# The last sample's chain cut in halves over VectorE and ScalarE, with its logits made twice

## The chip, the core and the metric

The kernel runs on one core of one Trainium2 chip. The metric is the device time of one execution in microseconds (us), lower is better. TensorE (PE in the profile) multiplies matrices and turns tiles around, and writes to PSUM; VectorE (DVE) and ScalarE (ACT) read PSUM and write to SBUF; GpSimd (POOL) works on SBUF only; SyncE (SP) issues nearly all DMAs. Each engine works through its own instructions in order, and the engines wait for each other through semaphores.

## What is computed

The reference is a network of two layers on 16 samples of 128 channels by 32 x 32 places (1024 tokens of 128 channels), all in float32:

```
x = x + linear_attention(ln_c(x));   t = tokens(x);  t = t + spectral_filter(ln_t(t))      # layer 0
x = x + conv_block(ln_c(x));         t = tokens(x);  t = t + routed_experts(ln_t(t))       # layer 1

conv_block(u):  relu(bn(conv3x3(relu(bn(conv3x3(u))))) + u)
routed_experts(t):                     # t: 16 x 1024 x 128, 64 experts, K = 8
  probs  = softmax(t @ gate_w.T + gate_b, over the 1024 tokens)
  topv, topi = the 8 largest of each expert's 1024 probabilities
  pooled = sum over those 8 tokens of topv * token              # 16 x 64 x 128
  out    = gelu(pooled @ weight1 + bias1) @ weight2 + bias2     # one expert, one pair of matrices
  result[topi] += topv * out
```

Only layer 1 matters here, and of it the last of the 16 samples: from its second convolution to the moment when its pooled tokens are there, without which no expert can start.

## The kernel before, in words

Layer 0 fills the first half of the time. Layer 1 has three stages.

**Samples.** Every sample b runs through some seventy named steps, from `even` (the inverse transform of layer 0's filter) to `channels_copy`; every second sample (odd b) also runs the routing of its pair (b-1, b): `logits`, `largest`, `exp`, `replace`, `gates`, `turn`, `turn_copy`, `pool`, `pool_copy`, `pooled`, `pooled_copy`. The steps are methods of the class `Routed`. A table gives each step an engine, a cost, a due time and what it waits for; `planned` makes one list of all steps of all samples out of it. The loop under `manual_schedule` calls the methods in that list's order, and on each engine the instructions stand as they were called. With its list the planner works on two or three samples at once: while sample b is in its second convolution, sample b-1 is in its routing.

**The steps of the last sample (b = 15) that matter**, with the lines of the profile:

- `sums2` (L1218, L1219), `mids2` (L1226), `rows2` (L1232): VectorE gathers the second convolution (PE, L1013) into `yo`.
- `resid` (L1272) and `last` (L1278): VectorE adds the residual, applies relu, and adds the sample's own `x` (the tile `xp`); 1024 elements each.
- `tokens2` (PE, L152): eight transposes turn `x` into tokens, into a PSUM tile `big`. `stats2` (DVE, L135): four `bn_stats`, for the mean and the variance of each token.
- `copy2` (ACT, L1291): copies the tokens into the SBUF tile `tt`. `variance2` (POOL, L1294), `root2` (ACT, L121 and L122) and `scales2` (DVE, L127 to L129 and L1090) make a scale and a shift for each token; `norm2` (ACT, L144, eight instructions) applies them to `tt` in place.
- `channels` (PE, L172) turns the normalised tokens back; `channels_copy` (ACT, L1312) copies them into `tk`.
- `logits` (PE, L1320): four matmuls, for two halves of 512 tokens and for both samples of the pair, into one `big` tile `pl` (experts of sample 14 on partitions 0 to 63, of sample 15 on 64 to 127).
- `largest` (DVE, L1328 to L1331): the eight largest logits of each row, and the shift for the exponential. `replace` (DVE, L1341): marks those eight in a copy `lr`. `exp` (ACT, L1335): exponential of `pl` into `eg`, with its sum. `gates` (DVE, L1344 and L1347): keeps the exponential where `lr` is marked; a reciprocal of the sum.
- `turn` (PE, L152), `turn_copy` (ACT, L1360): gates with tokens on partitions, in `gtt`. `pool` (PE, L1367): 16 matmuls of gates by tokens. `pool_copy` (DVE, L1374), `pooled` (PE, L1380), `pooled_copy` (DVE, L1384).

Two things run beside these steps. `keep` issues matmuls on the identity whose result nobody reads (`wm`, L165), so many behind a step as the dictionary `idle` says. And a PSUM tile is tracked as a whole: where two engines touch one `big` tile (two banks of PSUM), the later in program order waits for the earlier, also if both only read.

**Experts.** 16 groups of four experts: `hidden` (PE, L1555 for the bias and L1564; gelu on ACT, L1570), `turn` (PE, L1578; DVE, L1580), `output` (PE, L1589; DVE, L1594), `collect` (PE, L1600; DVE, L1601). The weights of a group are two halves of 1 MB; there are 32 halves, in a ring of 14 places. A half is loaded when the group before it in its place has been used (`load_half`). Ahead of the first group ScalarE makes `ob` (L1610, eight instructions: the second bias times each pair's `rs`) in the place of `lr`, and loads the table for gelu.

**Outputs.** Two matmuls by sample half spread the experts' results over the tokens (L1649), VectorE, or ScalarE and GpSimd, add them to `x` (L1656, L1657, L1659), and a DMA of 512 KB by sample writes them out (L1660). The gates of earlier pairs and ten of the samples come back from memory for this (`gt`, L1492; `xb`, L965). The loads of gates are issued behind `logits`, and wait for the places `tk` (free after `logits`) and `tt` (free after `pool`).

Of the kernel before, what the change touches and what calls it, by code (L numbers as in the profile page):

```python
# [8 lines left out]
F32 = mybir.dt.float32  # L9
AF = mybir.ActivationFunctionType  # L10
ALU = mybir.AluOpType
# [3 lines left out]
P = 128  # L15
B, C, H, W = 16, 128, 32, 32
N = H * W
# [52 lines left out]
def metaformer_kernel(ctx: ExitStack, tc: tile.TileContext, io: dict, out: bass.AP):  # L70
# [70 lines left out]
    def normalize(dst, src, r, nm, lo=0, hi=NT):  # L141

        for j in range(lo, hi):
            nc.scalar.activation(  # L144
                dst[:, j, :], src[:, j, :], AF.Identity,
                bias=nm[:, j : j + 1], scale=r[:, j : j + 1],
            )
# [29 lines left out]
    with ExitStack() as l0:  # L177
# [43 lines left out]
        with ExitStack() as a0:  # L221
# [121 lines left out]
            def big():  # L343
                return ps.tile([P, N], F32, name="big", tag="big", bufs=3)
# [6 lines left out]
            def small(shape, name):  # L351
                return work.tile(shape, F32, name=name, tag=name, bufs=5)
# [3 lines left out]
            class Attention:  # L356


                def __init__(self, b):
                    self.b = b  # L360
                    self.sts = small([P, 4, NT], "sts")
                    self.sts2 = small([P, 4, NT], "sts2")
                    self.ga = small([P, 4], "ga")
                    self.qs = small([P, 3], "qs")
                    self.ks = small([P, 2, NT * HEADS], "ks")

                def tokens(self):
                    if self.b + 2 < B:
                        load(self.b + 2)
                    self.x = xt[self.b]  # L370
                    self.pt = big().rearrange("p (j c) -> p j c", c=C)
                    transpose_in(self.pt, self.x)
# [45 lines left out]
                def channels(self):  # L418
                    self.px = big()
                    transpose_out(self.px, self.tok)  # L420
# [145 lines left out]
                def norm2(self):  # L566
                    normalize(self.ub, self.ub, self.sts2[:, 0], self.sts2[:, 3])
# [367 lines left out]
    with ExitStack() as c1:  # L935
# [83 lines left out]
        def big():  # L1019
            return ps.tile([P, N], F32, name="big", tag="big", bufs=2)  # L1020

        idle = {(13, "turn"): 4, (13, "pooled"): 8, (15, "logits"): 11, (15, "turn"): 1}

        def tokens(t):
            return t.rearrange("p (j c) -> p j c", c=C)
# [69 lines left out]
        class Routed:  # L1095
# [57 lines left out]
            def copy(self):  # L1153
                self.tok = work.tile([P, NT, C], F32, name="tok", tag="tok", bufs=1)
                nc.scalar.copy(self.tok, self.pt)
# [120 lines left out]
            def last(self):  # L1276
                xv = self.x.rearrange("p (n o) -> p n o", o=4)
                nc.vector.scalar_tensor_tensor(  # L1278
                    xv, self.yo.rearrange("p o n -> p n o"), 0.0, xv, ALU.max, ALU.add
                )  # L1280
# [5 lines left out]
            def stats2(self):  # L1286
                self.stats()
# [99 lines left out]
                )  # L1387


        table = (  # L1390
            ("yin", "SP", 2.4, 10207.4, "", "y", ""),
            ("even", "POOL", 1.37, 11971.6, "yin", "z", ""),
# [97 lines left out]
        def load_gates(pr, tag, bufs):  # L1490
# [4 lines left out]
            table, buffers, B, 240.92, lambda b, name: b % 2 == 0 and name in pairs,  # L1495
            lambda b, name: 0.6 if name == "yin" and b else 0.0,
        )
        with tc.manual_schedule(engines=PINNED | {mybir.EngineType.SP}):
            for b in range(2):
                load(b)  # L1500
            for n in range(2):
                nc.sync.dma_start(cw[n], cwd[n])
            bs = w1[:, C, :].rearrange("(k r i) h -> r k i h", r=2, i=EG)
            for r in range(2):
                nc.sync.dma_start(b1[r * E // 2 : (r + 1) * E // 2, :], bs[r])
            for j in range(2):
                nc.sync.dma_start(b2[j * E : (j + 1) * E, :], w2[:, HID, :])
            samples = [None] * B
            keep(ps, "cv", 26)
            for b, name in order:  # L1510
                if name == "yin":
                    if b > 1:
                        load(b)
                    continue
                if samples[b] is None:
                    samples[b] = Routed(b)
                arg = args.get(name, (name,))
                getattr(samples[b], arg[0])(*(
                    getattr(samples[b], a) if a in ("va", "vb") else a for a in arg[1:]
                ))  # L1520
                if name == "tokens2":
                    if b // 2 in AWAY:
                        nc.sync.dma_start(xd[b], samples[b].x)
                    if b % 2 == 0 and b // 2 - 1 in AWAY:
                        load_half(b // 2 - 1 - AWAY[0])
                keep(ps, "cv", idle.get((b, name), 0))
                if b == B - 1 and name == "inverse":
                    for h in range(5, 9):
                        load_half(h)
                elif b == B - 1 and name == "convc":  # L1530
                    load_half(9)
                elif b == B - 1 and name == "last":
                    for h in range(10, len(RING)):
                        load_half(h)
                elif b == B - 1 and name == "logits":
                    for pr in range(2):
                        load_gates(pr, "tk", 2)
                    for pr in range(2, 4):
                        load_gates(pr, "tt", 4)
# [276 lines left out]
```

## Time and profile before

The median of four runs is 1234.5 us (1231.87, 1233.5, 1235.51, 1237.07). The profiled execution is the last of these.

| | |
|---|---|
| profiled execution's own time | 1237.07 us |
| its span in the profile | 1235.3 us |
| busy share of the span: PE, PE's weight loads, DVE, ACT, POOL | 94%, 77%, 75%, 59%, 49% |
| mean granted clock of TensorE | 0.986 |
| DMA moved, mean over the span | 142 GB/s |
| last `sums2` of sample 15 begins (DVE, L1218) | 1113.37 us |
| first gelu begins (ACT, L1570) | 1146.80 us |
| first output DMA issued (SP, L1660) | 1211.28 us |

Times are from the start of the span. A row of a timeline gives start and duration of a group of like instructions, and in brackets how long the engine had idled before it and what ended the idling. A row of a table by stretches gives, for each engine, the busy time and (x) the number of instructions, then the clock that TensorE was granted (1.00 is full speed), the share of the 16 DMA engines that was busy, and GB/s.

### The profile page before, as it was taken

To read this page: it belongs to the slowest core of one execution; us is meant where nothing else is said; L and a number is where in the kernel's file an instruction comes from. 1 tells how busy PE (TensorE), PEld (TensorE's weight loads), DVE (VectorE), ACT (ScalarE), POOL (GpSimd) and SP (SyncE) were. 2 spreads that over 40 slices of the span, in tenths; PEclk is the share of its full clock that TensorE was granted. 3 is DMA by queue.
4 is the path that set the end of the run, shared out by engine and by line. 5 is a ranking of instruction groups with operands and counts; after the bars stand their busy time and mean duration, and the time that the engine had idled before them with its cause. 6 is when DMAs were issued, how large, how long until landed. Compare 5 with 4: busy or idle time off the path is not lost.

```text
span 1235.3 us, 34369 instructions
## 1 busy us (share of the span) xinstructions
PE 1162.6 (94%) x14376; PEld 952.3 (77%) x14376; DVE 929.4 (75%) x1944; ACT 725.2 (59%) x1420; POOL 602.0 (49%) x800
## 2 busy tenths in 40 slices
PE   7889999999998999999997999999999999998996
PEld 4676767777777999999996888888888888885443
DVE  5888888887776677777764789898898989884335
ACT  4777777776655777777761346555556555644211
POOL 2436454654568788888882434343333334320003
PEclk9989999999999999999998999999999999999998
DMA  7014435253445244444448412233332331416998
GB/s 281 24 31 152 137 98 166 91 165 118 137 136 180 84 137 141 140 135 138 140 141 285 116 52 66 81 94 119 119 105 86 102 103 51 154 34 239 353 404 334
DMA packets 91243, 175.14 MB, mean 142 GB/s; under 512 B 5968, under 2 KB 42064, under 8 KB 90448
## 3 DMA queue, kind: packets, MB, share of 16 engines
q1 hardware_dynamic: 90448, 170.46, 41.5%
q0 software_dynamic: 640, 2.49, 0.6%
q8 instruction: 113, 1.85, 0.6%
q14 instruction: 42, 0.34, 0.1%
HBM read 110.28 MB, written 62.65 MB: 140 GB/s over the span
## 4 chain that ended last, share of the span: by engine, by line
PE 53%; DVE 22%; issue 11%; ACT 5%; DMA 5%; POOL 3%; SPq 0%; POOLq 0%; ACTq 0%; DVEq 0%
PE pcv L1013 10%; PE pg L817 9%; PE py L841 9%; PE big L639 6%; DVE bst L135 4%; PE big L172 3%; PE big L152 3%; PE big L571 3%; PE big L451 2%; PE big L534 2%; PE big L433 2%; DVE abss L1256 1%; DVE xp L1278 1%; DVE xp L1140 1%; ACT tt L144 1%
## 5 line engine op out<-in xcount | busy, mean ns | idle before, releaser
L1013 PE MATMUL pcv<-v,cw 128*128 128x256 f32 x1152 | 258.2, 380 | 1.6 <-POOL v L1203 1.6
L1013 PEld LDWEIGHTS pcv<-v,cw 128*128 128x128 f32 x1152 | 214.7, 190 | 34.7 <-issue 4.9
L828 DVE COPY g<-pg 128x512 f32<-128x512 f32 x196 | 127.8, 683 | 69.8 <-PE pg L817 69.8
L830 ACT COPY g<-pg 128x512 f32<-128x512 f32 x316 | 161.1, 605 | 28.3 <-PE pg L817 27.5
L817 PE MATMUL pg<-ph,mst 32*128 32x128 f32 x4096 | 139.1, 278 | 1.4 <-DVE x L646 0.9
L817 PEld LDWEIGHTS pg<-ph,mst 32*128 32x128 f32 x4096 | 126.3, 186 | 15.5 <-DVE g L828 8.7
L841 PE MATMUL py<-g,v 128*32 128x128 f32 x4096 | 126.1, 276 | 2.8 <-POOL v L809 1.8
L841 PEld LDWEIGHTS py<-g,v 128*32 128x32 f32 x4096 | 109.1, 111 | 10.8 <-POOL v L809 2.3
L144 ACT ACTIVATE tok<-tok,sts 128x128 f32<-128x128 f32 x256 | 101.9, 480 | 17.0 <-DVE sts L1090 13.6
L135 DVE BATCH_NORM_STATS2 bst<-big 128x6 f32<-128x256 f32 x256 | 91.2, 418 | 20.8 <-PE big L152 11.7
L808 POOL TENSOR_TENSOR v<-xc 128x256 f32<-128x256 f32 x128 | 97.1, 783 | 13.1 <-DMA xc<-vd 12.2
L639 PE MATMUL big<-u,mu 128*128 128x128 f32 (+4 forms) x384 | 86.0, 380 | 0.0
L1203 POOL TENSOR_TENSOR v<-abss 128x256 f32<-128x256 f32 x64 | 49.1, 786 | 68.1 <-DVE abss L1199 56.7
L287 POOL TENSOR_TENSOR xf<-ab 128x256 f32<-128x256 f32 x34 | 24.8, 728 | 113.5 <-DVE ab L254 113.4
L1222 POOL TENSOR_TENSOR yo<-abss 128x256 f32<-128x256 f32 x32 | 23.5, 736 | 108.6 <-DVE abss L1218 108.6
L639 PEld LDWEIGHTS big<-u,mu 128*128 128x128 f32 x384 | 56.7, 191 | 18.0 <-issue 15.4
L571 PE MATMUL big<-wf,ub 128*128 128x256 f32 x256 | 63.3, 391 | 0.2
L144 ACT ACTIVATE tt<-tt,sts 128x128 f32<-128x128 f32 x128 | 51.1, 481 | 14.5 <-DVE sts L1090 14.5
L809 POOL TENSOR_SCALAR v<-v 128x256 f32<-128x256 f32 x64 | 55.1, 861 | 5.6
L476 POOL TENSOR_TENSOR ke<-ke,ks 128x1024 f32<-128x1024 f32 x16 | 30.6, 1915 | 55.0 <-DVE qs L484 43.4
L915 ACT COPY yt<-py 128x512 f32<-128x512 f32 x60 | 35.2, 586 | 32.6 <-ACT g L830 16.3
L571 PEld LDWEIGHTS big<-wf,ub 128*128 128x128 f32 x256 | 46.9, 193 | 9.0 <-ACT xn L424 3.0
(256 smaller groups left out, 2489.3 us busy)
## 6 DMA issues: line engine op xcount, KB each, us to landing
we<-in_weight SPq DMA_DIRECT2D x32, 1024.0 KB, 9.3
xc<-vd SPq DMA_DIRECT2D x64, 256.0 KB, 3.2
yd<-ys SPq DMA_DIRECT2D x32, 512.0 KB, 3.8
vd<-xf SPq DMA_DIRECT2D x15, 1024.0 KB, 5.1
y<-yd SPq DMA_DIRECT2D x15, 896.0 KB, 6.8
x<-in_x SPq DMA_DIRECT2D x16, 512.0 KB, 5.1
mi<-in_M_phi SPq DMA_DIRECT2D x16, 512.0 KB, 4.7
xd<-x SPq DMA_DIRECT2D x16, 512.0 KB, 6.4
```

Source lines behind the costliest of these rows:

```text
L135: nc.vector.bn_stats(bst[:, j : j + 2, :].rearrange("p j s -> p (j s)"), src[:, j : j + 2, :].rearrange("p j c -> p c j"),)
L144: nc.scalar.activation(dst[:, j, :], src[:, j, :], AF.Identity, bias=nm[:, j : j + 1], scale=r[:, j : j + 1],)
L571: nc.tensor.matmul(dst, self.ub[:, q, :], wf[:, q, :], start=True, stop=True)
L639: nc.tensor.matmul(self.pa[:, a:hi], mu[:, NF - 1 - si, tap, :], self.u[:, a - tap : hi - tap], start=(tap == 0), stop=(tap == KU - 1),)
L808: nc.gpsimd.tensor_tensor(vv[:, x, 1:, bs], e, o, op)
L809: nc.gpsimd.tensor_scalar(v[:, :, 0, bs], v[:, :, 2, bs], -1.0, None, ALU.mult)
L817: nc.tensor.matmul(pg[r][:, i], mst[rs, 4 * q + i, :], ph[rs, c, :], start=True, stop=True,)
L828: nc.vector.tensor_copy(dst, src)
L830: nc.scalar.copy(dst, src)
L841: nc.tensor.matmul(py[rows, x, kl, :], v[:, (x * NM + m) * JL + jl, 1 - ri : 3 - ri, :] .rearrange("p k b -> p (k b)"), g[:, ((x * 2 + ri) ...
L1013: nc.tensor.matmul(pc[:, i], wt[:, dy, k, :], v[:, k, dy * WT : dy * WT + HT], start=(dy == 0), stop=(dy == 2),)
L1203: nc.gpsimd.tensor_tensor(v[:, k, WT : WT + HT], self.ab[:, 0], self.ab[:, 1], op)
```

## The change

The change touches the last sample only (and, of samples 13 and 14, the place of some steps in the list). A class `Final` takes the place of `Routed` for b = 15.

- `resid` and `last` become one step that works in two halves of 512 elements, with the transposes of each half behind it; the statistics of the first half are taken ahead of the second half's transposes.
- `copy2` is gone: the normalisation reads PSUM and writes `tt`, five of eight instructions on VectorE, three on ScalarE.
- `channels` goes into two small PSUM tiles of one bank each; VectorE copies one, ScalarE the other.
- `logits` are made twice, into two tiles. The maximum and the replacement read one, the exponential the other. The maximum is taken over two halves and then over the 16 results.
- The gates are made, turned and copied in halves; ScalarE copies the first half, VectorE the second. `gtt` takes the place of `tok` instead of `lr`.
- Ten steps are moved in the list: `exp` ahead of `replace`, `root2` ahead of where `copy2` stood; of sample 13, `pool_copy` and `pooled` behind `stats2` of sample 15 and `pooled_copy` behind its `scales2`; of sample 14, `scales2` and `norm2` behind `mids2` of sample 15, `channels` behind its `tokens2`, `channels_copy` behind its `root2`.
- `idle`: 2 instead of 8 unread matmuls behind `pooled` of sample 13, and 7 instead of 11 behind the last `logits`.

In the built program, the instructions and waits of all engines are the same up to the last `sums2`. Behind it, the transposes of the second half wait for the first half's two `bn_stats`; ScalarE's three normalisations wait for VectorE's fifth; the first `max` waits for all four matmuls of the first logits; four of the eight `ob` stand ahead of ScalarE's copy of the gates, and wait for the second half of `gates`; the transposes of the second half of the gates wait for that copy, VectorE's copy of them too.

```diff
@@ -1019,7 +1019,7 @@
         def big():
             return ps.tile([P, N], F32, name="big", tag="big", bufs=2)
 
-        idle = {(13, "turn"): 4, (13, "pooled"): 8, (15, "logits"): 11, (15, "turn"): 1}
+        idle = {(13, "turn"): 4, (13, "pooled"): 2, (15, "logits"): 7, (15, "turn"): 1}
 
         def tokens(t):
             return t.rearrange("p (j c) -> p j c", c=C)
@@ -1385,6 +1385,110 @@
                     pooled[:, :E, 2 * pr : 2 * pr + 2],
                     self.pp.rearrange("p (j e) -> p e j", j=2),
                 )
+
+
+        halves2 = (slice(0, HALF), slice(HALF, N))
+
+        class Final(Routed):
+
+
+            def __init__(self, b):
+                super().__init__(b)
+                self.bst = work.tile([P, NT, 3], F32, name="bst", tag="bst", bufs=5)
+
+            def nothing(self, *_):
+                pass
+
+            resid = tokens2 = copy2 = channels_copy = turn = turn_copy = nothing
+
+            def count(self, h):
+                for j in range(4 * h, 4 * h + 4, 2):
+                    nc.vector.bn_stats(
+                        self.bst[:, j : j + 2, :].rearrange("p j s -> p (j s)"),
+                        self.pt[:, j : j + 2, :].rearrange("p j c -> p c j"),
+                    )
+
+            def flip(self, dst, src, h):
+                for j in range(4):
+                    nc.tensor.transpose(dst[:, j, :], src[:, 4 * h + j], ident)
+
+            def last(self):
+                v = nc.vector
+                self.pt = tokens(big())
+                xj = self.x.rearrange("p (j c) -> p j c", c=P)
+                for h in range(2):
+                    ns = slice(h * HT // 2, (h + 1) * HT // 2)
+                    yo = self.yo[:, :, ns]
+                    v.scalar_tensor_tensor(
+                        yo, yo, bn[:, 1, 1:2], self.p1[:, :, ns], ALU.add, ALU.add
+                    )
+                    xv = self.x[:, halves2[h]].rearrange("p (n o) -> p n o", o=4)
+                    v.scalar_tensor_tensor(
+                        xv, yo.rearrange("p o n -> p n o"), 0.0, xv, ALU.max, ALU.add
+                    )
+                    if h:
+                        self.count(0)
+                    self.flip(self.pt[:, 4 * h : 4 * h + 4], xj, h)
+
+            def stats2(self):
+                self.count(1)
+                self.m, self.q = self.bst[:, :, 1], self.bst[:, :, 2]
+                self.sts = small([P, 4, NT], "sts")
+
+            def norm2(self, i):
+                if i:
+                    return
+                self.tt = toks[self.b] = work.tile([P, NT, C], F32, name="tt", tag="tt", bufs=4)
+                r, nm = self.sts[:, 0, :], self.sts[:, 3, :]
+                for j in range(5):
+                    nc.vector.tensor_scalar(
+                        self.tt[:, j], self.pt[:, j], r[:, j : j + 1], nm[:, j : j + 1],
+                        ALU.mult, ALU.add,
+                    )
+                normalize(self.tt, self.pt, r, nm, 5, NT)
+
+            def channels(self):
+                tks[self.b] = work.tile([P, N], F32, name="tk", tag="tk")
+                for h, copy in enumerate((nc.vector.tensor_copy, nc.scalar.copy)):
+                    pu = ps.tile([P, 4, P], F32, name="pu", tag="cv", bufs=3)
+                    self.flip(pu, self.tt, h)
+                    copy(tks[self.b][:, halves2[h]], pu.rearrange("p j c -> p (j c)"))
+
+            def logits(self):
+                super().logits()
+                one = self.pl
+                super().logits()
+                self.pl, self.pl2 = one, self.pl
+
+            def exp(self):
+                one, self.pl = self.pl, self.pl2
+                super().exp()
+                self.pl = one
+
+            def largest(self):
+                v = nc.vector
+                self.top = work.tile([P, TOPK], F32, name="top", tag="top")
+                two = work.tile([P, 2 * TOPK], F32, name="two", tag="two", bufs=1)
+                for h in range(2):
+                    v.max(two[:, h * TOPK : (h + 1) * TOPK], self.pl[:, halves2[h]])
+                v.max(self.top, two)
+                self.ss = work.tile([P, 3], F32, name="sm", tag="sm")
+                v.tensor_tensor(self.ss[:, 0:1], self.top[:, 0:1], gb, ALU.add)
+                v.tensor_tensor(self.ss[:, 1:2], gb, self.ss[:, 0:1], ALU.subtract)
+
+            def gates(self):
+                self.pg = tokens(big())
+                self.gtt = work.tile([P, NT, P], F32, name="gtt", tag="tok", bufs=1)
+                gj = self.gt.rearrange("p (j c) -> p j c", c=P)
+                for h, copy in enumerate((nc.scalar.copy, nc.vector.tensor_copy)):
+                    cs, js = halves2[h], slice(4 * h, 4 * h + 4)
+                    nc.vector.scalar_tensor_tensor(
+                        self.gt[:, cs], self.lr[:, cs], LOW, self.gt[:, cs], ALU.is_le, ALU.mult
+                    )
+                    self.flip(self.pg[:, js], gj, h)
+                    copy(self.gtt[:, js], self.pg[:, js])
+                nc.vector.reciprocal(rs[:, self.pr : self.pr + 1], self.ss[:, 2:3])
+                gates[self.pr] = self.gt
 
 
         table = (
@@ -1495,6 +1599,22 @@
             table, buffers, B, 240.92, lambda b, name: b % 2 == 0 and name in pairs,
             lambda b, name: 0.6 if name == "yin" and b else 0.0,
         )
+
+        def move(op, ahead=None, behind=None):
+            order.remove(op)
+            order.insert(order.index(ahead or behind) + (ahead is None), op)
+
+        e, d = B - 1, B - 2
+        move((e, "exp"), ahead=(e, "replace"))
+        move((e, "root2"), ahead=(e, "copy2"))
+        move((d - 1, "pool_copy"), behind=(e, "stats2"))
+        move((d - 1, "pooled"), behind=(d - 1, "pool_copy"))
+        move((d - 1, "pooled_copy"), behind=(e, "scales2"))
+        move((d, "channels"), behind=(e, "tokens2"))
+        move((d, "channels_copy"), behind=(e, "root2"))
+        move((d, "scales2"), behind=(e, "mids2"))
+        move((d, "norm20"), behind=(d, "scales2"))
+        move((d, "norm21"), behind=(d, "norm20"))
         with tc.manual_schedule(engines=PINNED | {mybir.EngineType.SP}):
             for b in range(2):
                 load(b)
@@ -1513,7 +1633,7 @@
                         load(b)
                     continue
                 if samples[b] is None:
-                    samples[b] = Routed(b)
+                    samples[b] = (Routed if b + 1 < B else Final)(b)
                 arg = args.get(name, (name,))
                 getattr(samples[b], arg[0])(*(
                     getattr(samples[b], a) if a in ("va", "vb") else a for a in arg[1:]
```

## The prediction

> **What bounds the kernel now.** I read the busy times by stretches first (columns: length; busy time and instructions of PE, weight loads, DVE, ACT, POOL; granted clock; DMA share; GB/s).
>
> ```profile
> 1074.00:1112.00 38.00, 37.49 (x218) 30.97 (x216) 31.13 (x56) 18.28 (x33) 12.83 (x15) 1.00 0.09 29
> 1112.00:1147.00 35.00, 29.75 (x187) 18.74 (x186) 14.45 (x33) 17.43 (x38) 1.15 (x3) 0.95 0.68 238
> 1147.00:1203.00 56.00, 52.88 (x824) 27.62 (x824) 19.77 (x47) 9.36 (x16) 0.00 (x0) 1.00 1.03 390
> ```
>
> Up to 1112 TensorE is full. From 1147 to 1203 the experts run with the DMA engines full. The 35 us between have no full engine: VectorE and ScalarE are busy less than half, and much of PE's time is unread matmuls. So the timelines of single engines come next, where the idle time in brackets tells who waits for whom. First VectorE, then ScalarE, then PE:
>
> ```profile
> 1132.74 1.23 DVE L1328 MAX8 top<-big 128x8 f32<-128x1024 f32 x1 [7.65 <-PE big L1320]
> ...
> 1134.35 1.22 DVE L1341 MATCH_REPLACE8 lr<-top,big 128x1024 f32<-128x1024 f32 x1
> 1136.89 1.23 DVE L1344 SCALAR_TENSOR_TENSOR eg<-lr,eg 128x1024 f32<-128x1024 f32 x1 [1.32 <-ACT eg L1335]
> ...
> 1142.70 0.35 DVE L1374 TENSOR_SCALAR pl<-pp,rs 128x128 f32<-128x128 f32 x1 [4.51 <-PE pp L1367]
> ```
>
> ```profile
> 1122.77 1.01 ACT L1291 COPY tt<-big 128x1024 f32<-128x1024 f32 x1 [3.03 <-DVE bst L135]
> 1123.68 0.31 ACT L121 ACTIVATE sts<-bst,eps 128x8 f32<-128x8 f32 x1
> ...
> 1125.13 3.19 ACT L144 ACTIVATE tt<-tt,sts 128x128 f32<-128x128 f32 x8 [0.91 <-DVE sts L1090]
> 1128.88 1.01 ACT L1312 COPY tk<-big 128x1024 f32<-128x1024 f32 x1 [0.57 <-PE big L172]
> 1135.65 1.11 ACT L1335 ACTIVATE eg<-big,sm 128x1024 f32<-128x1024 f32 x1 [5.75 <-DVE lr L1341]
> ...
> 1143.04 2.45 ACT L1610 ACTIVATE ob<-b,rs 128x128 f32<-128x128 f32 x8 [2.67 <-PE pp L1367]
> 1145.50 1.28 ACT L1570 ACT_TABLE_LOAD   x1
> 1146.80 0.60 ACT L1570 ACTIVATE hs<-ph 128x512 f32<-128x512 f32 x1
> ```
>
> ```profile
> 1121.16 3.62 PE L165 MATMUL wm<-ident 128*128 128x256 f32 x16
> 1125.68 3.17 PE L172 MATMUL big<-ident,tt 128*128 128x128 f32 x8 [0.90 <-ACT tt L144]
> 1128.78 3.93 PE L1320 MATMUL big<-tk,gw 128*64 128x512 f32 x8
> ```
>
> One chain: each engine waits for the one before it. Stalls to see: the copy ahead of L121, the exponential behind the replacement (both read `big`), and `ob` and the table load, which end 0.94 after the first `hidden` (1145.86).
>
> The clock rows (PE's busy time alone, clock, DMA) show why the logits took so long, and PE's waits from 1143 on that the weights set the end:
>
> ```profile
> 1128.00:1129.00 1.00, 0.94 (x3) 0.62 0.06 25
> 1129.00:1130.00 1.00, 1.00 (x3) 0.50 0.00 0
> 1131.00:1132.00 1.00, 1.00 (x5) 0.68 0.00 0
> 1132.00:1133.00 1.00, 1.00 (x5) 1.00 0.00 0
> ```
>
> ```profile
> PE peo L1589 <- DMA we<-in_weight: 2.3, 1, 2.3
> ```
>
> **The change, part by part.** All from the profiled execution; negative is time gained on the chain.
>
> 1. Sample 14's four scale operations (0.76 by their starts) go behind `mids2`. Today `sums2` waits behind them until 1113.37, though its convolution ends at 1112.16 and VectorE is free at 1112.22. New: `sums2` 1112.25, two at 0.72; `mids2` to 1114.71; scales to 1115.47; `rows2` at 1115.47 instead of 1116.01: **-0.54**. The normalisation of 14 then starts at 1115.6 instead of 1113.49 and ends at 1118.8; its `channels` are due at 1121.1, so 2.3 us hide it.
> 2. `resid` and `last` in halves: today 1.32 + 1.95 = 3.27. A 512-element operation that waits for its forerunner takes 0.72 (`sums2`); half of `last` 0.97 to 1.05 (half of 1.95, plus the fixed part). 0.72 + 0.97 + 0.72 + 1.05 = 3.46: **+0.19**. Bound: as fast as unstrided 0.72, that is 0.6 less; nothing slower than 1.95 for a half, which no row suggests.
> 3. Statistics: today 2.68 from the end of `last` to the end of four `bn_stats` (eight transposes, then 1.43). New: two 0.67 (they begin before `last` has drained), 0.11, four transposes 0.66 (half of 1.07 and a wait), two 0.76: 2.20: **-0.48**. Only VectorE's first pair overlaps nothing, since the second transposes wait for it.
> 4. No copy ahead of L121: 0.99 between statistics and L121 becomes 0.08: **-0.91**. The roots (0.58) and scales stay. `pool_copy` of 13 fits under the roots.
> 5. Normalisation: today 3.22 (eight at 0.385, the last 0.48). New: `pooled_copy` of 13 first, 0.20; five on VectorE; wait 0.10; then ScalarE's three, 1.25, since they wait. No row has this VectorE form. Nearest: L1374 alone 0.34, a row of eight L1631 at 0.26 each. I take 0.26: 4 x 0.26 + 0.34 = 1.38. Bounds 1.0 (half of a 256-element operation's 0.34 between starts) to 1.75. Sum 2.93: **-0.29** (-0.67 to +0.08). `channels_copy` of 14 (1.0) runs on ScalarE meanwhile.
> 6. ScalarE copies 512 instead of 1024 elements: 0.59 (L1214) for 1.01: **-0.42**. VectorE's copy is done 1.5 us earlier.
> 7. Logits. Today, from ScalarE's copy (1129.89) to `max` 2.85; at full clock sample 13's logits took 1.92 from the same point (1100.63 to 1102.55). New: PE starts at about 1126.45, when the eight transposes are through; the first half is done when ScalarE's copy lands at 1127.37, one matmul stays: about 1.1 at full clock, `max` at 1128.45: **-1.75**, of which 0.93 is today's half clock. The second logits (1.75, to 1130.2) lie beside `largest`.
> 8. `max` to `gates`: today 4.15. New: two halves and 16 results, 0.60 + 0.69 + 0.20, then two of 0.20: the shift is there at 1.86. Exponential 1.30 beside the replacement (end 3.10): gates at 3.28: **-0.87**. If the `max` of a half cost as much as a whole one, +1.2; as cheap as half without a fixed part, -0.1.
> 9. `gates` to the end of `pool`: today 5.73. New: two halves end at 1.32; four `ob` at 0.306, 1.23, stand ahead of ScalarE's copy; copy 0.6; transposes 0.66; VectorE's copy 0.65 beside 0.45 unread matmuls and half of `pool` (0.98); other half 0.98: about 6.25: **+0.52**. The halves give nothing here, as each waits for the other.
> 10. End of `pool` to first gelu: today 4.18. `ob` and table load are done before (about 1138.3): 1.07 of bias, `pooled`, copy, `hidden`: 2.80: **-1.38**.
>
> Sum: -0.54 + 0.19 - 0.48 - 0.91 - 0.29 - 0.42 - 1.75 - 0.87 + 0.52 - 1.38 = **-5.93**; first gelu at about 1140.9. The first `hidden` itself comes 5.0 earlier.
>
> **Does it reach the end?** The experts run into the weights: DMA share 0.99 to 1.06 from 1150 to 1205, and a wait of 2.3 for the last half. That stream starts with the loads behind the first and second `hidden` (issued at 1145.91 and 1149.2), which come 5.0 and 5.9 earlier; before, the DMA engines are free (0.26 in 1140 to 1145). SP's queue keeps its order: loads of gates behind the last reading of `tk` come at 1130.2 for 1132.7, behind `pool` at 1138.1 for 1142.6. So nearly all of it arrives; I take 5.5. Against the profiled execution 1237.07 - 5.5 = 1231.6. That one is 2.6 above the median and had the half clock in the logits; other executions may not, so of those 0.93 I give up 0.4: 1234.5 - 5.1 = **1229.4**.
>
> **Rivals.**
>
> - *Half clock in the new logits.* Clock 0.50 lasted one stretch of 3.4 (1128.3 to 1131.7), and again 1203.4 to 1206.8, 22 such stretches later: a fixed grid. In the 3.4 before the first, PE had eight spaced transposes; before the second, at least 1.1 us of matmuls did not avert it. New: between the two unread matmuls (end 1123.4) and the logits (1126.45) lie 3.05 us with eight transposes, about as thin. A stretch of the grid falls just there in perhaps one execution of five. Price: logits of 1.75 for 3.5, less what waits anyway: 1.55, so 1231.0. [...]
> - *It does not reach the end.* The stream of weights is bound by bytes; if its start were set by something that does not move, the wait of 2.3 would grow to 7.8: 1234.5. Against: the free DMA engines before 1145.9. 0.12.
> - *Slower: half clock through the whole routing.* PE has from the logits to `pool` 3.5 of logits, 3.2 of unread matmuls (14 at 0.226) standing ahead of `turn`, and 3.9 more up to the bias; each stretch at 0.50 loses 1.7. The first costs 1.55; two more eat the rest of 5.5; from the fourth in a row it is slower. Throughout, PE reaches `turn` at 1126.45 + 13.4 = 1139.9, `hidden` at 1150.6: first gelu 6.0 later than today, 1240.5. For: 9 unread matmuls instead of 19. Against: in both rows above the clock was back after one stretch. 0.05.
> - *The two logits do not run apart*: the exponential still ends behind the replacement. Price 1.2: 1230.6. 0.06.
>
> **How the numbers follow.** Forecast 0.62, the others as given. About 0.3% (3.7 us) is what a measurement of this kernel can tell from no change; faster means below 1230.8. The forecast alone falls there by 0.85, half clock and undivided logits by half: 0.62. Slower: the third rival and a part for what I overlook in a chain of ten steps: 0.11. Same: 0.27. Range: 1226.4 (all 5.9, VectorE's low bounds in 5 and 8, and a run of the lower kind) to 1234.5 (nothing arrives).
>
> **What would show it.** Right: L121 right behind the last `bn_stats`; `max` with an idle time of about 3 instead of 7.65; the exponential beginning before the replacement ends; first gelu behind PE, not behind the table load; the wait for the last weights 2 to 4. Wrong: ScalarE's copy of `gtt` the longest wait, a clock of 0.50 between 1123 and 1138, or first gelu early and the first output DMA not.

## The result, and the profile after

| | median | runs | lowest to highest |
|---|---|---|---|
| kernel before | 1233.47 us | 69 | 1228.29 to 1240.56 |
| changed kernel | 1230.29 us | 43 | 1226.18 to 1236.93 |

The ratio of the times is 0.9971, with a 95% interval of 0.9962 to 0.998: 2.5 to 4.7 us faster. The profiled execution of the changed kernel took 1229.26 us, with a span of 1227.3 and a mean clock of 0.991. The forecast was 1229.4.

Read first the engine that waited longest before. VectorE's timeline of the changed kernel (start, duration, group, in brackets the idle time ahead of it and what ended it):

```profile
1126.72 1.30 DVE L1473 MAX8 two<-big 128x8 f32<-128x512 f32 x2 [2.72 <-PE big L1320]
...
1128.61 1.22 DVE L1341 MATCH_REPLACE8 lr<-top,big 128x1024 f32<-128x1024 f32 x1
1129.94 1.29 DVE L1485 SCALAR_TENSOR_TENSOR eg<-lr,eg 128x512 f32<-128x512 f32 x2
1133.83 0.69 DVE L1489 COPY gtt<-big 128x512 f32<-128x512 f32 x1 [2.60 <-PE big L1413]
```

The wait ahead of the maximum is 2.72 instead of 7.65, and nothing stands between the replacement and the gates any more. A new wait of 2.60 has come, ahead of VectorE's copy of the gates. ScalarE's timeline says why:

```profile
1119.99 0.30 ACT L121 ACTIVATE sts<-bst,eps 128x8 f32<-128x8 f32 x1 [3.19 <-DVE bst L1406]
...
1123.24 1.16 ACT L144 ACTIVATE tt<-big,sts 128x128 f32<-128x128 f32 x3 [1.81 <-DVE tt L1444]
...
1128.70 1.11 ACT L1335 ACTIVATE eg<-big,sm 128x1024 f32<-128x1024 f32 x1 [3.30 <-DVE sm L1477]
...
1131.27 1.28 ACT L1730 ACTIVATE ob<-b,rs 128x128 f32<-128x128 f32 x4 [1.36 <-DVE eg L1485]
1132.46 0.56 ACT L1489 COPY gtt<-big 128x512 f32<-128x512 f32 x1
...
1138.84 0.60 ACT L1690 ACTIVATE hs<-ph 128x512 f32<-128x512 f32 x1 [2.51 <-PE ph L1684]
```

L121 stands directly behind the statistics; the exponential begins at 1128.70, 0.09 behind the replacement's begin and beside it; the four `ob` stand ahead of the copy, as forecast; the first gelu waits for PE and no longer for the table. From the reciprocal of sample 13 (VectorE, L1347), the last common instruction, to the first gelu it is 34.73 us before and 28.75 now: **5.98 less, where the forecast's sum was 5.93**. The median gained 3.2. So the study is about the difference.

Part of the answer lies 54 us later. The longest of PE's waits from 1140 on (total, times, longest):

```profile
PE peo L1709 <- DMA we<-in_weight: 1.8, 1, 1.8
```

And the table by stretches at the same place, cut at 3.41 us (columns as in the prediction):

```profile
1192.01:1195.42 3.41, 1.63 (x35) 1.21 (x36) 0.57 (x3) 0.00 (x0) 0.00 (x0) 1.00 1.02 414
1195.42:1198.84 3.42, 3.42 (x13) 3.06 (x12) 1.79 (x7) 0.00 (x0) 0.00 (x0) 0.50 1.03 420
1198.84:1202.25 3.41, 3.35 (x16) 1.66 (x17) 0.84 (x3) 0.00 (x0) 0.00 (x0) 1.00 0.69 281
```

PE waits 1.8 us for the last weights, is busy for only 1.63 of that stretch, and has half the clock for the whole next one. There the last transposes and unread matmuls stand, on the way to the outputs.

### The profile page after: what moved, and what is told of

It reads as the page before. It is cut to its first block, busy times and chain, and to the rows that moved or that the text cites. A ratio compares the mean times of both kernels' runs of the same rounds, so it can differ in the third digit from the quotient of the medians.

```text
span 1227.3 us, 34351 instructions
## 1 busy us (share of the span) xinstructions
PE 1153.2 (94%) x14364; PEld 944.7 (77%) x14364; DVE 933.2 (76%) x1956; ACT 721.7 (59%) x1414; POOL 602.2 (49%) x800
## 3 DMA queue, kind: packets, MB, share of 16 engines
q1 hardware_dynamic: 90448, 170.46, 41.7%
## 4 chain that ended last, share of the span: by engine, by line
PE 54%; DVE 22%; issue 10%; ACT 6%; DMA 5%; POOL 2%; SPq 0%; POOLq 0%; ACTq 0%; DVEq 0%
PE pcv L1013 10%; PE pg L817 10%; PE py L841 10%; PE big L639 6%; DVE bst L135 4%; PE big L172 3%; PE big L152 3%; PE big L571 3%; PE big L451 2%; PE big L534 2%; PE big L433 2%; DVE abss L1256 1%; DVE xp L1278 1%; DVE xp L1140 1%; ACT ub L550 1%
## 5 line engine op out<-in xcount | busy, mean ns | idle before, releaser
L144 ACT ACTIVATE tt<-tt,sts 128x128 f32<-128x128 f32 x120 | 47.8, 481 | 13.9 <-DVE sts L1090 13.9
```

The lines of the kernel that those rows point to most:

```text
L144: nc.scalar.activation(dst[:, j, :], src[:, j, :], AF.Identity, bias=nm[:, j : j + 1], scale=r[:, j : j + 1],)
```

## The experiments

**Theory.** The chain's gain is whole and arrives at the start of the experts. Part of it is given back at their end: PE waits for the weights' stream, and the thin stretch costs half a clock. **Rivals.** The first profile of before was a bad one; the fewer unread matmuls cost clock in the routing; the end doesn't follow the experts' start.

What the profiles measured of each kernel (us; the last two columns together are the experts and what follows them):

| kernel | begin to reciprocal of 13 | to first gelu | to last `peo` | to first `pfy` |
|---|---|---|---|---|
| before | 1112.07 | 34.73 | 54.66 | 6.55 |
| before_again | 1110.77 | 34.27 | 53.22 | 5.06 |
| after | 1110.09 | 28.75 | 54.19 | 6.73 |
| after_again | 1110.38 | 28.73 | 54.19 | 7.77 |
| after_third | 1109.24 | 28.73 | 54.30 | 6.46 |
| unread_back | 1118.44 | 28.72 | 54.74 | 6.49 |
| one_logits | 1111.46 | 33.06 | 53.09 | 5.05 |
| after_tail | 1111.30 | 28.72 | 53.75 | 5.05 |
| after_tail_2 | 1109.47 | 28.74 | 54.77 | 5.05 |
| before_tail | 1111.49 | 35.05 | 53.62 | 4.93 |
| before_tail_2 | 1108.42 | 33.73 | 55.21 | 4.94 |
| apart | 1108.20 | 27.11 | 53.10 | 5.04 |
| apart_tail | 1108.17 | 27.12 | 53.62 | 5.06 |
| whole_gates | 1108.26 | 31.04 | 53.07 | 5.07 |

**before_again, after_again, after_third**: no edit.

> The kernel before, unchanged, profiled a second time: a control. Theory (all of the chain's gain arrives, and single executions differ by where stretches of half clock fall): from the reciprocal of sample 13 (L1347) to the first gelu 34.7 us as in the first profile if a half-clock stretch falls into the logits again, 33.8 if none does; a median of about 1233.5 with a ratio of 1.000. Rival (part of the gain of 6.0 that the two profiles show is only that the first profile of before was a bad one): clearly less than 33.8, towards 32.

> The changed kernel, unchanged, profiled a second time: a control. Theory: from the reciprocal of sample 13 to the first gelu 28.7 us again, if no stretch of half clock falls there, and some 30 if one does; the first gelu to the end of the span 88.5; median about 1230.3. Rival (the change has more half clock, since it has 9 unread matmuls instead of 19 there): a clock of 0.50 between the last statistics and the first gelu, and 30 to 32 us. Rival (the end does not move with the experts' start): the wait for the last weights above 4 instead of 1.8.

> The changed kernel once more, on the chip and in the minutes of the next two. Theory (a wait for the last weights and a half clock behind it in nearly every execution): 28.7 us from the reciprocal to the first gelu, 54.2 to 54.8 from there to the last peo, 6.5 to 7.8 from the last peo to the first pfy, and the kernel before ahead of nothing: ratio 0.997. Rival (both profiles were chance): 5.1 from the last peo to the first pfy.

Measured: 1235.86, 1230.31 and 1230.92 us (12 runs each), beside 1233.29, 1233.29 and 1231.34 of the kernel before; ratios 1.0019 (0.9994 to 1.0044), 0.9976 (0.9952 to 1.0001), 0.9991 (0.9964 to 1.0018). The ratio expected of the third, 0.997, was missed, and so was the stretch from the first gelu to the end of the span in after_again: 89.7 instead of 88.5, with two stretches at half clock behind the wait. The chain is the same to 0.02 in all three profiles of the changed kernel, and before has 34.27 beside 34.73: the chain's gain was no chance. In all three of the changed kernel the wait of 1.8 to 1.9 and the half clock behind it are there; before had them in the first profile and not in the second. There PE's timeline shows the last `peo` waiting only 0.8, put down to a copy of VectorE:

```profile
1198.26 1.08 PE L1589 MATMUL peo<-we,ht 128*32 128x128 f32 x32 [0.82 <-DVE ot L1601]
```

The last weights land 0.13 before it begins, so they come in time, if barely. Last `peo` to first `pfy` is 5.06 there, and 6.5 to 7.8 where the clock was halved.

**unread_back**:

```diff
-        idle = {(13, "turn"): 4, (13, "pooled"): 2, (15, "logits"): 7, (15, "turn"): 1}
+        idle = {(13, "turn"): 4, (13, "pooled"): 5, (15, "logits"): 7, (15, "turn"): 1}
```

> The changed kernel with five unread matmuls instead of two behind the transposition of 13's pooled rows, that is in the 1.5 us in which PE waits for the normalisation (each about 0.47 us by the rows of the changed kernel, so 1.4 more, in time that PE has free). Theory: nothing is gained, 1230.3 within 1 and 28.7 us from the reciprocal to the first gelu. Rival (the thinner stretch costs half clock in the logits in a good part of the executions, which is why the medians differ by 3.2 to 3.6 and not by 5): 1.0 to 1.5 faster than the changed kernel, and a higher mean clock.

1229.44 us, ratio 0.9969 (0.9943 to 0.9995), chain 28.72. Nothing gained that can be measured; against the 1230.3 of the changed kernel it is -0.9, and the interval (-2.8 to 2.4) is too wide to exclude the rival's 1.0 to 1.5 by the time. The profiles speak against its size: of the nine with the change and only two unread matmuls there, one has half clock in the logits (whole_gates, below), at 1.5. (This profile has its begin 8 us longer; it holds five of its half-clock stretches before 700 us.)

**after_tail, after_tail_2, before_tail, before_tail_2**: the changed kernel and the kernel before, each twice, with

```diff
                 if g > 1:
                     collect(g - 2, og.pop(g - 2))
+                if g == ng:
+                    keep(ps, "cv", 3)
                 if g:
                     og[g - 1] = output(g - 1, ht)
```

> The changed kernel with three unread matmuls (0.47 us each by their row, 1.4 in all) between the last transposition of the experts' results and the last 32 matmuls peo, where PE waits 1.8 us for the last weights in both profiles of the changed kernel. Theory (the chain's gain reaches the start of the weights' stream, but PE now waits for the last weights with its array so idle that the clock is halved for the next window of 3.41 us, which costs 1.5 to 2.7 between the last peo and the first pfy): the last peo starts when it did (54.2 after the first gelu), from it to the first pfy 5.1 instead of 6.7 and 7.8, no clock of 0.50 between 1190 and 1210, median 1.5 to 2 below the changed kernel, 1228.5. Rival (the half clock there has another cause, or the unread matmuls hold up the last ones): 6.5 or more from the last peo to the first pfy, or the last peo later, 1230 to 1231.5.

> The kernel before with the same three unread matmuls. Theory: of its two profiles one had the wait (2.3) and the half clock behind it, the other a wait of 0.8 and none; so about half of its executions gain 1.5 and the others lose 0.6: median within 1 of the kernel before, 1232.5 to 1233.3, and the changed kernel with the three then leads it by 4 to 5 and not by 3.2. Rival (the tail has nothing to do with the missing part of the gain): the two kernels with unread matmuls stand as far apart as the two without, 3.0 to 3.5.

> The changed kernel with the three unread matmuls, a second time, now beside the changed kernel itself, since the first run told its lead only against the kernel before. Theory: 5.05 from the last peo to the first pfy again and 1.5 to 2.5 faster than the changed kernel of the same minutes. Rival (the unread matmuls give in the end nothing, as the first comparison with the kernel before says: 0.9971 with and 0.9971 to 0.9976 without): within 0.7 of it.

> The kernel before with the three unread matmuls, a second time. The first was 4.9 above the kernel before, which no view of its profile shows: the three cost at most 1.4. Theory A (a loaded program differs from another load of the same by 2 to 3 us, as the unchanged kernel before did with 1235.86 beside 1233.29): this time between 1229 and 1235 where the kernel before has 1231 to 1233. Theory B (the added matmuls cost the kernel before something themselves): 4 to 5 above it again.

Measured: after_tail 1228.15 beside 1231.8 of before (0.9971; 0.9955 to 0.9986), after_tail_2 1227.2 beside 1231.34 (0.9963; 0.994 to 0.9986) and beside 1230.92 of the changed kernel. PE's timeline of after_tail at the place:

```profile
1192.26 1.46 PE L165 MATMUL wm<-ident 128*128 128x256 f32 x6
1193.77 1.08 PE L1709 MATMUL peo<-we,ht 128*32 128x128 f32 x32
...
1198.82 1.56 PE L1771 MATMUL pfy<-gt,ob 64*128 64x512 f32 x6
```

The unread matmuls fill the wait here; in after_tail_2 a wait of 1.1 for the weights is left behind them. In both profiles `pfy` follows 5.05 behind the last `peo`, and the clock is full from 1190 to 1216. So the half clock behind the wait is gone, as the theory has it. What that is worth in the time is less sure. Side by side, in the last series, it is 3.7 (interval 0.9 to 7.0), more than the 1.5 to 2.5 expected, and outside the rival's 0.7. Over all runs of the study the changed kernel has 1230.3 (67 runs) and 1227.8 with the three matmuls (24): -2.5, interval -3.9 to -1.0. (Intervals over all runs come from resampling the medians, as if the runs were one series.) But the runs come from several series, and the kernel before had 1233.3 to 1233.5 in those with most of the 67 and 1231.3 to 1231.8 in those with the 24. Measured against the kernel before of its own series, the changed kernel has -3.2, -3.0 and -0.4, with the three matmuls -3.7 and -4.1; so part of the 2.5 may belong to the series.

The kernel before was the surprise: before_tail 1236.81 (ratio 1.004; 1.0024 to 1.0056) and before_tail_2, the same program, 1229.43 (0.9976; 0.9953 to 0.9999). No view of the first one's profile shows 5 us, and the second run does not have them. So theory A: a series of runs can sit some us off as a whole, and what puts it there is not settled. Together they have 1232.7 (24 runs) beside 1232.9 of before (174 runs). With the end covered in both kernels, the changed one leads by 4.9 (2.2 to 8.2) over all runs, where the chains differ by 5.0 to 6.3; without, by 2.6 (1.5 to 3.5). But the 4.9 is made of two leads that lie far apart, 8.7 beside before_tail and 2.2 beside before_tail_2. So neither the theory's 4 to 5 nor the rival's 3.0 to 3.5 is shown.

**one_logits**: `Final.logits` and `Final.exp` are left out, so that there is one `pl`.

> The changed kernel with one set of logits, which maximum, exponential and replacement all read; the exponential stands ahead of the replacement as in the changed kernel. Theory: the exponential and the replacement run one behind the other, max to gates 4.3 to 4.5 instead of 3.2, so 1.2 later there; the four ob operations now all stand behind ScalarE's copy, so gates to the end of pool is shorter by up to 0.4, but ob and the table load (1.2 + 1.2 + 1.28) then end after the first hidden: the first gelu 1.5 to 2.2 later, about 1232. Rival (VectorE and ScalarE read one tile side by side, or the second logits push the rest back): no later than the changed kernel, 1230.

1230.63 us, ratio 0.9972 (0.9947 to 0.9996): the 1.5 us expected are not seen in the time, which is the rival's (no later than 1230), though not by its reason. In the profile the step is as the theory expected, 4.54 from maximum to gates instead of 3.22; in VectorE's timeline the replacement waits for the exponential:

```profile
1131.29 0.09 DVE L1341 MATCH_VALUE_LOAD lr<-top,big 128x8 f32 x1 [1.32 <-ACT eg L1335]
```

Behind it more came than was expected. PE has nothing to do for 2.23 ahead of the transposed gates, and two stretches at half clock follow, as its table by stretches shows:

```profile
1130.80:1134.21 3.41, 1.18 (x7) 0.57 (x7) 2.58 (x4) 0.55 (x3) 0.00 (x0) 1.00 1.01 402
1134.21:1137.63 3.42, 3.42 (x10) 1.28 (x8) 0.71 (x2) 2.54 (x8) 0.00 (x0) 0.50 0.22 90
1137.63:1141.04 3.41, 3.41 (x33) 3.24 (x32) 0.05 (x1) 1.69 (x2) 0.00 (x0) 0.50 0.00 0
```

`pool` takes 3.63 instead of 1.97. This is the mechanism of the slower rival, in a relative of the kernel. Of the 4.3 that its chain lost, 2.8 came back behind the first gelu, where there was no wait for weights.

**whole_gates**: `Final.gates` is left out, and `turn` and `turn_copy` are real again.

> The changed kernel with gates, transposition and copy of the last pair whole again, as the kernel before has them; all else stays. Theory: gates to the end of pool 5.3 to 5.7 instead of 6.1, but all eight ob and the table load (2.45 and 1.28) now follow ScalarE's copy and end behind the first hidden again, pool end to first gelu 4.0 to 4.2 instead of 2.8: 29.5 to 29.9 from the reciprocal to the first gelu. So the halves pay only by letting half of ob through early. Rival (the halves themselves shorten the stretch): 30.5 or more; or (they cost): below 28.7.

1226.99 us in one execution. Gates to the end of `pool` 5.8, from there to the gelu 3.9, together 9.7 instead of 8.9: the halved gates gain 0.8, by letting `ob` and the table go early, as the theory said. The chain of 31.04, which by itself would fit the rival's 30.5 or more, holds 1.5 beyond these 0.8, and that is the rival *half clock in the new logits*, met at last. VectorE's timeline, at the maximum:

```profile
1126.39 1.30 DVE L1473 MAX8 two<-big 128x8 f32<-128x512 f32 x2 [4.22 <-PE big L1320]
```

and the stretch of the clock's grid in which the logits fell, with the one before it:

```profile
1118.97:1122.38 3.41, 2.77 (x11) 1.24 (x9) 2.99 (x10) 1.61 (x4) 0.00 (x0) 1.00 1.06 407
1122.38:1125.79 3.41, 3.41 (x10) 1.13 (x12) 0.00 (x0) 0.77 (x2) 0.00 (x0) 0.50 0.32 130
```

4.22 instead of 2.72, so 1.5; forecast 1.55. One profile of the ten with the change in them had it there.

**apart, apart_tail**: the halves in tiles of their own, the second also with the three unread matmuls ahead of the last `peo`. The core of the edit:

```diff
-                self.pt = tokens(big())
+                self.pt = [
+                    ps.tile([P, 4, P], F32, name="pth", tag="cv", bufs=3) for _ in range(2)
+                ]
...
-                for j in range(5):
+                for j in range(4):
...
-                self.pg = tokens(big())
...
+                    pg = ps.tile([P, 4, P], F32, name="pg", tag="cv", bufs=3)
+                    self.flip(pg, gj, h)
...
+                self.ob = work.tile([P, NPAIR, C], F32, name="ob", tag="lr", bufs=1)
+                for q in range(NPAIR):
+                    nc.scalar.activation(self.ob[:, q], b2, AF.Identity, scale=rs[:, q : q + 1])
```

> The changed kernel with the halves in PSUM tiles of their own (tokens of sample 15 and transposed gates each in two tiles of one bank instead of one of two), four of eight normalised by VectorE instead of five, all ob operations behind ScalarE's copy, 5 unread matmuls instead of 7 behind the logits. Theory (the halves of the changed kernel gain nothing at three places because both lie in one tile and wait for each other): second transposes behind the second half of last, not behind bn_stats, 0.6; ScalarE's normalisation beside VectorE's and not behind it, 0.9 to 1.2; gates to the end of pool 4.2 to 4.6 instead of 6.1: from the reciprocal of sample 13 to the first gelu 25.0 to 25.8 instead of 28.7. The time falls by less, 1.5 to 3, as the wait for the last weights comes on top: 1227.5 to 1229. Rival (the two engines hold each other up in PSUM anyway, or ob and the table load become the end): 27.5 to 28.7 and no faster than 1230.

> Both: the halves in tiles of their own and the three unread matmuls in front of the last peo. Theory: the two gains add up, first gelu 25.0 to 25.8 behind the reciprocal and 5.1 from the last peo to the first pfy: 1225.5 to 1227.5. Rival (the weights' stream takes back what the chain gains): the same time as the changed kernel with the three unread matmuls alone, with the wait for the last weights 3 longer.

apart 1224.86 us (0.9949; 0.9934 to 0.9965), apart_tail 1223.28 (0.9938; 0.9919 to 0.9957; 6 runs), beside 1231.8 of before: **the fastest version is 8.5 us below the kernel before**, and its ratio lies clear of the changed kernel's 0.9962 to 0.998. Both are over 2 us below the range expected of them, and yet the chain is 27.11, not 25.0 to 25.8. Statistics 1.58 instead of 2.18 gave the 0.6 expected, normalisation 1.54 instead of 2.99 more than the 0.9 to 1.2. But 0.7 went again behind it: 1.38 to the end of ScalarE's copy, which now waits for the eight transposes (0.79, for PE), and 1.69 from there to the maximum, instead of 1.01 and 1.31. And gates to the end of `pool` is 5.29, not 4.2 to 4.6, and the gelu 3.29 behind it, not 2.78, because the bias matmuls of the first `hidden` now stand elsewhere in PE's order. Its timeline:

```profile
1127.47 0.66 PE L1413 MATMUL pg<-ident,eg 128*128 128x128 f32 x4
1128.06 1.04 PE L1681 MATMUL ph<-b,ident 32*32 32x512 f32 x2
1129.03 0.65 PE L1413 MATMUL pg<-ident,eg 128*128 128x128 f32 x4
```

One of them splits the two halves' transposes, and more of them are left for behind `pool`. That would be the next edit; it was not made. Apart is faster than the changed kernel by 5.4 (3.8 to 7.1) over all runs, by 2.7 to 5.2 if each is set against the kernel before of its own series (0.9949 beside 0.9971 to 0.9991), with a chain shorter by 1.6. Two more parts are seen in its profile: no wait for weights (53.10 and 5.04), and a begin of 1108.2, with two half-clock stretches in the whole execution (660.0 to 666.8, and from 1213.0 on, when PE has no work left; mean clock 0.994). Whether its other executions have them too is not shown. Since apart's profile has no wait at the end, what its sister with three more matmuls gains beyond it is not told apart.

## Why the prediction was right, and where it wasn't

**The steps.** Measured in the profile of after, from the same marks as in the prediction (us, negative is gained):

| step | forecast | measured |
|---|---|---|
| 1 scales of 14 moved | -0.54 | -0.53 |
| 2 `resid`, `last` in halves | +0.19 | +0.28 |
| 3 statistics | -0.48 | -0.50 |
| 4 no copy ahead of L121 | -0.91 | -0.95 |
| 5 normalisation | -0.29 | -0.23 |
| 6 half the copy | -0.42 | -0.56 |
| 7 logits | -1.75 | -1.54 |
| 8 maximum to gates | -0.87 | -0.93 |
| 9 gates to end of `pool` | +0.52 | +0.39 |
| 10 end of `pool` to gelu | -1.38 | -1.40 |

The sum is nearer than its terms, which is partly luck: misses of up to 0.2 go both ways. The largest are in 7 (1.31 from ScalarE's copy to the maximum, not 1.1) and 6. In 5 VectorE's five took 1.68, near the upper bound of 1.75 (0.34 each, like L1374 alone, and not like the group of eight that I took), but the other parts were shorter. Where the halves give nothing, the program showed it ahead of time: a wait for a whole tile; apart took it away and gained 2.0 at the two places.

**The step that failed** is "nearly all of it arrives; I take 5.5". The stream of weights begins with the first gelu in the changed kernel and 0.88 ahead of it before, so it gains 5.1 of the 6.0 in the first pair of profiles; that I had. But I then let the end follow the stream at no cost. From the first gelu to the issue of the last weights it was 41.25 to 41.31 in the changed kernel's three profiles and 41.7 and 40.0 in before's two; PE could have had the last `peo` at 53.1, as in one_logits, whole_gates and apart, and had it at 54.2 to 54.3. That is 1.1, and the half clock behind the wait 1.4 to 2.7. I had seen the same half clock in the first profile of before and charged it to no one, and had named a wait of 2 to 4 for the last weights a sign of being right (it was 1.8). The kernel before pays the same in one of its two profiles (54.66 and 6.55), so what the change loses here is a matter of how often, which so few profiles don't tell.

The time came out near all the same, and that is luck: the gain forecast, 5.1, is 1.9 more than the 3.2 measured, and the 1234.5 that I started from (four runs) is 1.0 above the 1233.47 of 69 runs. The two misses take from each other, and 0.9 is left.

The 0.4 that I gave up for the half clock in the logits of before was too much: three of its four profiles had it there (34.3 to 35.1; the fourth, without, 33.73). A typical pair is thus 5.5 to 6 apart in the chain; the ends of the profiled executions give back 1.5 (61.2 in the mean of three against 59.7 in the mean of two). The 1.5 rests on the second profile of before, with 58.3; the first has 61.2, and in that pair nothing is given back. That leaves 4 to 4.5, and the result is 3.2 between the medians, 3.6 by the ratio: about 1 us stays unexplained, less than two series of one program differ by. Why the stream of weights takes 40.0 in some executions and 41.3 or more in others, of the same program too, is open as well.

**The rivals.** Half clock in the logits: real, priced rightly, and met in one profile of ten. Its chance of 0.15 was my estimate, a little under the one execution in five taken for the grid's phase; the one in ten fits it. Not reaching the end: wrong in its reason, for the start of the stream moved by 5.1 and the wait was 1.8 and not 7.8; part of the gain was lost there by a mechanism that it didn't name. Half clock through the routing: not in the changed kernel, but seen in one_logits. Logits that do not run apart: no, 1.32 gained there.

## What to carry to other kernels

Follow a saved stretch to the next thing that something else sets, here the last load of a stream, and ask what PE does while it waits: a wait of 1.8 us cost up to 2.7 more at half clock, and with three matmuls that nobody reads the half clock was gone in both profiles. Halves on two engines need tiles of their own wherever waits go by tile, as here (2.0 in apart), and the order that a planner gives the fillers can decide whether the halves meet (in apart 1.04 of bias matmuls stand between them). Compare profiles from a common instruction on: the chain repeated to 0.02 us, where the whole time of one program moved by 7 between two series.

## What the runs showed of the hardware

**A grid of 3.413 us.** In the profile of before half clock (0.50) begins at 278.31, at 1128.23 and at 1203.32 and lasts 3.41 us each time; from the first of these to the last it is 271 times 3.413, from the second 22 times. The stretches that begin at 66.69 and 660.61 last 6.83. Within each of the 14 profiles every stretch at half clock begins at one phase of such a grid, to within 0.01; from execution to execution the phase differs. Each profile cut by its own grid into stretches of 3.413 us, of those at full clock from 10 us on:

| PE busy in the stretch (us) | stretches | next one at half clock |
|---|---|---|
| under 1.5 | 54 | 53 |
| 1.5 to 1.6 | 13 | 0 |
| 1.6 to 2.4 | 168 | 14 |
| over 2.4 | 4650 | 2 |

Busy time here has modelled ends, and spaced transposes count too long, which blurs the rows: in before each of the eight of L172 counts 0.33 us where they begin 0.38 apart, and 0.11 where they come in a row. The third row has 14 at half clock where the second has none. Counted as work, the same stretches part better. Take the columns that PE's matmuls move in a stretch, each matmul weighted by the rows times the columns of its weights over 128 x 128, the largest weights in the traces: of 67 stretches under 1500 columns 62 had half clock behind them, of 68 with 1500 to 1800 seven, of 4750 with more none. The one ahead of the half clock in whole_gates, with PE busy for 2.77, has 1408, and PE's longest idle time in it is 0.46; the one ahead of the half clock in the logits of before, with PE busy for 2.22, has 865. So in these profiles it is how little work a stretch holds that goes with half clock behind it, and not the longest idle time; in which stretch a thin place falls differs from execution to execution with the grid's phase.

**It goes with the spread.** Of the 44 executions of the changed kernel's first series, each with a known mean clock, those at 0.991 and 0.992 took 1227.6 in the mean, those at 0.985 to 0.987 took 1232.2. One stretch of 3.41 us at half clock takes 3.41 / 2 / 1228 = 0.0014 off the mean clock, so these groups lie some three stretches apart, at 1.7 us each (an estimate, half of 3.41) about the 4.6 us between them. That the stretches are all of the cause is not shown.
